# Two layers of graph attention on one core: where VectorE multiplies the context with the reciprocals

## The chip, the core and the metric

The kernel runs on one core of a Trainium2 chip. The core has engines with an instruction queue each, which work at the same time and wait for one another by semaphores: TensorE (PE, with the weight loads shown apart as PEld), VectorE (DVE), ScalarE (ACT), GpSimd (POOL) and SyncE (SP), which issues all of this kernel's DMAs. Inside a queue, instructions run strictly in the order in which the program wrote them. The metric is the device time of one execution in microseconds (us), the median of several runs.

## The reference

Two layers over x, of 8 elements (batch) x 2048 nodes x 256 features, with one 0/1 matrix `adj` of 2048 x 2048, each followed by a residual and a layer norm.

```python
# layer 0: per element, 4 heads of 64; keys in 8 chunks of 256
scores = einsum('bhnd,bhjcd->bhnjc', q, kc) / sqrt(Dh)
scores = clip(scores, -10, 10)
scores = where(mask == 0, -10, scores)
attn = softmax(scores, axis=-1)            # over the 256 keys of a chunk
ctx = einsum('bhnjc,bhjcd->bhnd', attn, vc)   # summed over the chunks
out = layernorm(ctx @ Wo.T + bo + x) * gamma + beta
x = layernorm(x + out)
# layer 1: per element, all 2048 keys
e = leaky_relu(s_i[:, :, None] + s_j[:, None, :], 0.2)
attention = softmax(where(adj > 0 or eye, e, -inf))
x = layernorm(x + elu(attention @ (x @ W)))
```

In layer 0 every chunk of 256 keys has a softmax of its own, so a chunk's part of the context is divided by that chunk's own sum, and the eight quotients are added.

## The kernel before

All arithmetic is in float32. Queries are taken in blocks of 512 (`ib`, four of them per element `b`), keys in chunks of 256 (`j`, eight of them). The main loop runs over J, the 8 x 4 x 8 = 256 triples (b, ib, j), and each J has two halves. A half is called a *beat*: it handles 128 keys against 512 queries for all heads, in two score tiles of 128 x 1024.

The order of the work is written out by hand. In a beat of the main loop the program writes, in this order:

1. `begin_beat` for layer 1: the exponentials of the steps that are due (`weights`, L727 on ACT), and with them the running sum of the weights (`acc`, L734 and L736 on POOL); the first instruction of new steps (`low`, L714 on ACT); and the second one of the steps begun a beat ago (`leaky`, L718 on DVE).
2. Layer 0's scores (L882 on PE), the clip against the mask (L893 on DVE, from PSUM in place), and the exponentials (L897 on ACT).
3. `middle_of_beat`: layer 1's mask (`edges`, L723 on DVE).
4. For the J before this one: the products of its exponentials with the values (L948 on PE). In the first half that is the denominators (part 2, against ones) and half the features, in the second the rest. ACT copies them out of PSUM: the features to `un` (L956), the denominators to `ds` (L962).
5. `end_beat`: layer 1's product (L746 on PE) and one step each of the generators in `ahead` (the preludes, which prepare layer 1 for an element; their row maxima are L438 on DVE) and `fins` (the output projection L357 with its norms, layer 1's end, and others). It then calls what stands in `agenda` for this beat; in the first element that is not over, and in the beats after the last scores, it calls the agenda ahead of the products and generators.

Denominators take a detour, since every head's row must be spread over 32 partitions. A DMA folds `ds` into the small tile `dc` (L964), DVE takes its reciprocal (`inverse`, L970), a DMA writes it to DRAM (L972), and a DMA reads it back spread over the partitions as `r` (`spread`, L976). Then `scaled` multiplies `un` by `r` on DVE (L983; L981 for a block's first chunk, which writes `ctxT` itself) and POOL adds the product to the context `ctxT` (L984).

From the second element on, `inverse` and `spread` stand at the end of the first half's beat and `scaled` at the end of the first half of the next J, two beats later. There the agenda holds `scaled` of one J in front of `inverse` of the next J, so that DVE's queue reads: ..., product, reciprocal, then the second half's L718, L893 and L723. In the first element, in which layer 1 does not run yet, all three come later.

A block's output projection may start in the beat after the one noted in `ctx_done`. Layer 1 takes 1.5 steps a beat, alternately one and two, of 128 keys against 512 queries; it begins when an element's layer 0 is done and its prelude has prepared it, and its weight tiles `w` have five buffers. `un` has two buffers.

Of the kernel before, what the change touches and what calls it, by code (L numbers as in the profile page):

```python
# [28 lines left out]
def tile_adj_attention__then__gat(  # L29
# [309 lines left out]
    ctx_done = {}  # L339
    fins = []  # L340
# [363 lines left out]
    class Step:  # L704
# [20 lines left out]
        def weights(self):  # L725
            k, c = self.k, self.c
            nc.scalar.activation(self.w, self.w, AF.Exp)  # L727
            if k["b"] == B - 1:
                return
            if c == 0:  # L730
                k["w0"] = self.w
            elif c == 1:
                k["acc"] = two.tile([P, IB], F32, tag="acc", name=f"acc{self.name}")
                nc.gpsimd.tensor_add(k["acc"], k.pop("w0"), self.w)  # L734
            else:
                nc.gpsimd.tensor_add(k["acc"], k["acc"], self.w)  # L736
# [65 lines left out]
    l1_live = True  # L802
    ahead = [prelude(b) for b in range(B - 1)] + [last_prelude(B - 1)]
    lows, edged, weighted = [], [], []
    agenda = {}
    beat = 0
    credit = 0.0
    RATE, LAST_RATE = 1.5, 1.3
# [1 line left out]
    def l1_open():  # L810
        return lows or edged or weighted

    def at(when, fn):
        agenda.setdefault(when, []).append(fn)

    def begin_beat(rate):
        nonlocal l1_live, credit, lows, edged, weighted, leaking
        weighted, edged = edged, []
        for s in weighted:
            s.weights()  # L820
        leaking, lows = lows, []
        credit = min(credit + rate, 2.0)
        while l1_live and credit >= 1.0:
            s = next(l1, False)
            if s is False:
                l1_live = False
            elif s is None:
                break
            else:
                credit -= 1.0  # L830
                lows.append(s)
                s.low()
        for s in leaking:
            s.leaky()

    def middle_of_beat():
        nonlocal edged
        for s in leaking:
            s.edges()
        edged = leaking  # L840

    def end_beat():

        nonlocal weighted
        if beat < 2 * NIB * NCH or beat >= 2 * total:
            for fn in agenda.pop(beat, []):
                fn()
        for s in weighted:
            s.product()
        weighted = []  # L850
        for gens in (ahead, fins) if beat < 2 * total else (fins, ahead):
            for g in list(gens):
                if next(g, g) is g:
                    gens.remove(g)
        for fn in agenda.pop(beat, []):
            fn()
# [14 lines left out]
    prev = None  # L871
# [28 lines left out]
    for J in range(total + 1):  # L900
        b, ib, j = J // (NIB * NCH), J // NCH % NIB, J % NCH
# [4 lines left out]
        for half in range(2):  # L906
            c = 2 * j + half
# [7 lines left out]
            if ahead_sc is not None:  # L915
                exponentials(cur, c, 0, ahead_sc)
            begin_beat(RATE if b < B - 1 else LAST_RATE)
            if live:

# [16 lines left out]
            early = J < NIB * NCH  # L936
            if prev is not None:
                if half == 0:

                    pool, tag = (one, "hr") if early and J % 3 == 2 else (two, "un")  # L940
                    prev["un"] = pool.tile([P, 2, IB], F32, tag=tag, name=f"un{prev['name']}")
                for part in ((2, 0), (1,))[half]:
                    m = ps_m.tile([P, IB], F32, tag="m", name=f"u{prev['name']}_{part}")
                    for i in range(2):
                        pc = 2 * prev["j"] + i
                        for h in range(H):
                            f0 = h * D + part * DH
                            nc.tensor.matmul(  # L948
                                m[h * DH : (h + 1) * DH, :],
                                prev["v"][pc // TPB][:, pc % TPB, f0 : f0 + DH] if part < 2 else ones[:, 0:DH],  # L950
                                prev["es"][2 * i + h // 2][:, h % 2, :],
                                start=(i == 0),
                                stop=(i == 1),
                            )
                    if part < 2:
                        nc.scalar.copy(prev["un"][:, part, :], m)  # L956
                    else:

                        ds = two.tile([P, IB], F32, tag="ds", name=f"ds{prev['name']}")
                        nc.scalar.copy(ds, m)  # L962
                        dc = two.tile([P, IB // DH], F32, tag="dc", name=f"dc{prev['name']}")
                        nc.sync.dma_start(  # L964
                            out=dc, in_=ds.rearrange("(h m) (n w) -> h m n w", m=DH, n=DH)[:, 0, :, :]
                        )
                        prev["dc"] = dc

                        def inverse(p=prev):
                            nc.vector.reciprocal(p["dc"], p["dc"])  # L970
                            p["rd"] = dram3.tile([H, IB], F32, tag="rd", name=f"rd{p['name']}")
                            nc.sync.dma_start(out=p["rd"].rearrange("h (m w) -> (h m) w", m=DH), in_=p["dc"])  # L972

                        def spread(p=prev):
                            p["r"] = two.tile([P, IB], F32, tag="r", name=f"r{p['name']}")
                            nc.sync.dma_start(out=p["r"], in_=p["rd"].unsqueeze(1).to_broadcast([H, DH, IB]))  # L976

                        def scaled(p=prev):
                            r2 = p["r"].unsqueeze(1).to_broadcast([P, 2, IB])
                            if p["j"] == 0:  # L980
                                nc.vector.tensor_mul(p["ctxT"], p["un"], r2)  # L981
                            else:
                                nc.vector.tensor_mul(p["un"], p["un"], r2)  # L983
                                nc.gpsimd.tensor_add(p["ctxT"], p["ctxT"], p["un"])  # L984
                            if p["j"] == NCH - 1:
                                ctx_done[p["b"], p["ib"]] = beat
                            if p["j"] == NCH - 3:
                                fins.append(fin(p["b"], p["ib"], p["ctxT"]))

                        lag = 1 if early else 0  # L990
                        at(beat + lag, inverse)
                        at(beat + lag, spread)
                        at(beat + 2 + 2 * lag, scaled)

            end_beat()
            if half == 1:
# [6 lines left out]
            beat += 1  # L1003
        prev = cur if live else None

    while agenda or fins or ahead or l1_live or l1_open():
        begin_beat(1.0)
        middle_of_beat()
        end_beat()
        beat += 1  # L1010
# [44 lines left out]
```

## Time and profile before

| what | value |
|---|---|
| time, median of 3 runs | 4385.68 us (4385.07 to 4389.45) |
| the profiled execution | 4386.54 us, its span 4384.7 us |
| mean granted TensorE clock | 0.979 |
| DMA traffic | 415.63 MB, mean 95 GB/s |
| reciprocals L970 | 256, of 0.25 us each |
| products L983 and L981 | 224 and 32; L983 has a mean of 1238 ns |
| context adds L984 | 224, mean 2535 ns |

A profile's row reads: line, engine, operation, output<-inputs with their shapes, count | busy us, mean ns of one | idle time of the engine just before, and what ended most of it. In a timeline the columns are start and duration in us, engine, line, operation, operands and count, and in brackets the idle time before and what ended it; neighbouring instructions of one line are merged. In the rows of windows the columns are the window, its length, and each engine's busy time with its number of instructions. A row of waits names who waited and for whom: us in total, times, the longest.

### The profile page before, as it was taken

The page shows a single profiled execution, that of the slowest core. Times are in us where ns is not written, and L with a number is a line of the kernel's source. Part 1 is how long each engine was busy: PE and PEld are TensorE (multiplying, and loading weights), DVE is VectorE, ACT ScalarE, POOL GpSimd, SP SyncE. Part 2 cuts the span into 40 slices and gives each one's busy share as a digit, 9 for nine tenths or more (in the row PEclk, how much of TensorE's full clock was granted, in tenths as well). Part 3 has the DMA queues.
Part 4 walks back from the last instruction along what each step waited for, and adds up shares of the span by engine and source line. Part 5 has one row for each costly group of instructions (what it writes and reads, how often), then busy time and mean ns, then how long its engine had stood idle before and what let it go on. Part 6 is the DMA issues. An engine that isn't in the chain of part 4 may idle for free.

```text
span 4384.7 us, 61166 instructions
## 1 busy us (share of the span) xinstructions
PE 4055.8 (92%) x23053; PEld 1913.0 (44%) x23053; DVE 3417.1 (78%) x4530; ACT 2555.5 (58%) x3842; POOL 1759.3 (40%) x901
## 2 busy tenths in 40 slices
PE   8889989999899999999899998999989999899767
PEld 3223334454345534454344543445434454344456
DVE  5876589965898668976699766996579965888777
ACT  5655556665566556666566665566556665555546
POOL 0222235543455434444245442554325542354420
PEclk9999999999999999999999999999999999999889
DMA  5554232223332133321333223222232222322321
GB/s 163 172 174 149 73 114 86 84 72 95 93 97 82 56 108 102 100 75 47 108 103 98 74 74 105 83 95 80 72 105 84 89 78 65 117 83 81 123 73 58
DMA packets 257642, 415.63 MB, mean 95 GB/s; under 512 B 85441, under 2 KB 120513, under 8 KB 256449
## 3 DMA queue, kind: packets, MB, share of 16 engines
q1 hardware_dynamic: 257344, 411.71, 30.7%
q8 instruction: 181, 2.97, 0.3%
q14 instruction: 117, 0.95, 0.1%
HBM read 340.66 MB, written 68.88 MB: 93 GB/s over the span
## 4 chain that ended last, share of the span: by engine, by line
PE 57%; DVE 23%; ACT 7%; DMA 7%; issue 5%; POOL 1%; SPq 0%; DVEq 0%; ACTq 0%; POOLq 0%
PE u L948 17%; PE sc L882 14%; PE us L746 12%; DVE sc L893 6%; DVE fb L438 3%; DVE w L718 3%; PE pv L275 3%; PE pk L256 3%; ACT e L897 3%; DMA dc<-ds 2%; PE pq L256 2%; DVE w L723 2%; PE po L357 2%; PE pw L398 2%; PE us L761 1%
## 5 line engine op out<-in xcount | busy, mean ns | idle before, releaser
L893 DVE SCALAR_TENSOR_TENSOR sc<-sc,mk 128x1024 f32<-128x1024 f32 x1024 | 1205.8, 1222 | 523.1 <-PE sc L882 375.0
L897 ACT ACTIVATE e<-sc 128x1024 f32<-128x1024 f32 x1024 | 1032.7, 1021 | 951.8 <-DVE sc L893 926.5
L882 PE MATMUL sc<-qT,kT 64*128 64x512 f32 x4096 | 1038.7, 622 | 71.8 <-ACT e L897 68.6
L984 POOL TENSOR_TENSOR ctxT<-ctxT,un 128x1024 f32<-128x1024 f32 x224 | 567.9, 2535 | 1135.6 <-DVE un L983 1099.8
L948 PE MATMUL u<-e,v 128*32 128x512 f32 x8192 | 982.8, 597 | 0.0
L746 PE MATMUL us<-wh,w 128*128 128x256 f32 x3584 | 883.0, 396 | 89.5 <-ACT w L727 68.2
L746 PEld LDWEIGHTS us<-wh,w 128*128 128x128 f32 x3584 | 669.8, 194 | 432.5 <-ACT w L727 119.7
L736 POOL TENSOR_TENSOR acc<-acc,w 128x512 f32<-128x512 f32 x392 | 600.0, 1531 | 548.1 <-ACT w L727 537.6
L882 PEld LDWEIGHTS sc<-qT,kT 64*128 64x128 f32 x4096 | 344.3, 186 | 581.3 <-issue 313.7
L718 DVE SCALAR_TENSOR_TENSOR w<-ab,sj,w 128x512 f32<-128x512 f32 x512 | 576.5, 1147 | 6.1 <-ACT w L714 6.1
L948 PEld LDWEIGHTS u<-e,v 128*32 128x32 f32 x8192 | 240.6, 110 | 659.8 <-issue 500.9
L948 PE MATMUL u<-e,ones 128*32 128x512 f32 x4096 | 498.4, 605 | 0.0
L723 DVE TENSOR_TENSOR w<-w,mk 128x512 f32<-128x512 f32 x512 | 458.5, 916 | 45.6 <-DMA mk<-mask 43.1
L438 DVE CUSTOM_DVE_ANT_0 fb<-sj_row,fb 128x1024 bf16<-128x1024 f32 x240 | 383.7, 1609 | 4.5 <-DMA fb<-far 4.5
L956 ACT COPY un<-u 128x512 f32<-128x512 f32 x512 | 300.7, 587 | 108.8 <-PE u L948 100.1
L714 ACT ACTIVATE w<-ab,sj 128x512 f32<-128x512 f32 x512 | 352.3, 715 | 9.9 <-POOL acc L734 5.2
L727 ACT ACTIVATE w<-w 128x512 f32<-128x512 f32 x512 | 308.8, 629 | 83.6 <-DVE w L723 83.2
L983 DVE TENSOR_TENSOR un<-un,r 128x1024 f32<-128x1024 f32 x224 | 277.2, 1238 | 43.6 <-DMA r<-rd 23.1
L948 PEld LDWEIGHTS u<-e,ones 128*32 128x32 f32 x4096 | 107.5, 110 | 352.7 <-issue 286.5
L970 DVE RECIPROCAL dc<-dc 128x16 f32<-128x16 f32 x256 | 63.5, 248 | 149.3 <-DMA dc<-ds 137.3
L962 ACT COPY ds<-u 128x512 f32<-128x512 f32 x256 | 148.6, 580 | 18.5 <-PE u L948 15.5
L357 PE MATMUL po<-WT_o,ctxT 128*128 128x256 f32 x512 | 127.4, 405 | 33.3 <-POOL ctxT L984 29.2
(112 smaller groups left out, 3078.7 us busy)
## 6 DMA issues: line engine op xcount, KB each, us to landing
r<-rd SPq DMA_DIRECT2D x256, 256.0 KB
mk<-mask SPq DMA_DIRECT2D x120, 512.0 KB
fb<-far SPq DMA_DIRECT2D x240, 256.0 KB
xT_k<-in_xT_dram SPq DMA_DIRECT2D x32, 512.0 KB
raw<-in_adjT_dram SPq DMA_DIRECT2D x32, 512.0 KB
rawf<-in_adj_dram SPq DMA_DIRECT2D x32, 512.0 KB
x<-in_x_dram SPq DMA_DIRECT2D x32, 512.0 KB
h_d<-y SPq DMA_DIRECT2D x32, 512.0 KB
```

What stands on the lines that cost most here:

```text
L438: nc.vector.tensor_tensor_reduce(out=fb, in0=row, in1=fb, scale=1.0, scalar=2 * FAR * 0.999, op0=ALU.add, op1=ALU.max, accum_out=dst,)
L714: nc.scalar.activation(self.w, k["ab"][:, 1, :], AF.Identity, bias=k["sj"][:, 1, c : c + 1])
L718: nc.vector.scalar_tensor_tensor(self.w, k["ab"][:, 0, :], k["sj"][:, 0, c : c + 1], self.w, ALU.add, ALU.max)
L723: nc.vector.tensor_tensor(self.w, self.w, self.k["mks"][self.c // HT][:, self.c % HT, :], ALU.min)
L727: nc.scalar.activation(self.w, self.w, AF.Exp)
L736: nc.gpsimd.tensor_add(k["acc"], k["acc"], self.w)
L746: nc.tensor.matmul(k["us"][:, t, :], self.w[:, ts(t, P)], k["wh"][c // TPB][:, c % TPB, 0:F], start=(first and t % 2 == 0), stop=last, ski ...
L882: nc.tensor.matmul(sc[:, h, :], kTs[b][n // TPB][h * D : (h + 1) * D, hp, ts(n % TPB, P)], qT[h * D : (h + 1) * D, hp, :], start=True, sto ...
L893: nc.vector.scalar_tensor_tensor(sc, sc, -CLIP, cap, ALU.max, ALU.min)
L897: nc.scalar.activation(e, sc, AF.Exp)
L948: nc.tensor.matmul(m[h * DH : (h + 1) * DH, :], prev["v"][pc // TPB][:, pc % TPB, f0 : f0 + DH] if part < 2 else ones[:, 0:DH], prev["es"] ...
L984: nc.gpsimd.tensor_add(p["ctxT"], p["ctxT"], p["un"])
```

## The change

`scaled` leaves the end of the beat for all chunks of which the denominators are made after the first element's scores. It is kept in a dictionary of its own, `scaling`, and is called in `begin_beat` of the next beat, behind all `leaky` calls of that beat and so in front of its clips. The running sum of layer 1's weights is split from `weights` into `sums`, which `begin_beat` calls after that; on GpSimd the context add therefore still comes in front of the same beat's weight adds. `ctx_done` is set one lower for the moved calls, so that the output projection is released in the same beat as before. Nothing else moves, and no instruction is added or taken away.

```diff
         def weights(self):
             k, c = self.k, self.c
             nc.scalar.activation(self.w, self.w, AF.Exp)
+
+        def sums(self):
+            k, c = self.k, self.c
             if k["b"] == B - 1:
                 return
             if c == 0:
...
-    agenda = {}
+    agenda, scaling = {}, {}
...
         for s in leaking:
             s.leaky()
 
+        for fn in scaling.pop(beat, []):
+            fn()
+        for s in weighted:
+            s.sums()
+
     def middle_of_beat():
...
                             if p["j"] == NCH - 1:
-                                ctx_done[p["b"], p["ib"]] = beat
+                                ctx_done[p["b"], p["ib"]] = beat if p["early"] else beat - 1
...
                         lag = 1 if early else 0
+                        prev["early"] = early
                         at(beat + lag, inverse)
                         at(beat + lag, spread)
-                        at(beat + 2 + 2 * lag, scaled)
+                        if early:
+                            at(beat + 2 + 2 * lag, scaled)
+                        else:
+                            scaling[beat + 3] = [scaled]
...
-    while agenda or fins or ahead or l1_live or l1_open():
+    while agenda or scaling or fins or ahead or l1_live or l1_open():
```

## The prediction

> **What bounds the kernel now.** I read the page's busy row, then the windows of one element (elements after the first repeat every 527 us; I use the third, 1005 to 1532 us), then what the reciprocals wait for, then the timeline around them.
>
> ```profile
> PE 4055.8 (92%) x23053; PEld 1913.0 (44%) x23053; DVE 3417.1 (78%) x4530; ACT 2555.5 (58%) x3842; POOL 1759.3 (40%) x901
> ...
> L718 DVE SCALAR_TENSOR_TENSOR w<-ab,sj,w 128x512 f32<-128x512 f32 x512 | 576.5, 1147 | 6.1 <-ACT w L714 6.1
> L983 DVE TENSOR_TENSOR un<-un,r 128x1024 f32<-128x1024 f32 x224 | 277.2, 1238 | 43.6 <-DMA r<-rd 23.1
> ```
>
> ```profile
> core 0: us, PE busy (x) PEld busy (x) DVE busy (x) ACT busy (x) POOL busy (x), PEclk, DMA share, GB/s
> 1005.00:1080.00 75.00, 72.48 (x439) 30.40 (x435) 38.97 (x58) 48.00 (x77) 23.05 (x11) 1.00 0.31 93
> 1080.00:1155.00 75.00, 62.83 (x415) 21.04 (x415) 62.01 (x88) 39.60 (x58) 23.57 (x10) 1.00 0.42 128
> 1155.00:1330.00 175.00, 168.05 (x947) 83.03 (x945) 168.18 (x206) 107.36 (x162) 92.95 (x48) 0.98 0.32 95
> 1330.00:1532.00 202.00, 198.51 (x1095) 103.03 (x1093) 147.85 (x192) 120.56 (x186) 93.40 (x51) 1.00 0.21 64
> ```
>
> PE is the bound, but not alone. From 1155 to 1330, where layer 1 runs beside the prelude's maxima (L438), DVE is as full as PE (168 of 175). In the first 150 us layer 1 stands still and PE idles 15 us in few, single waits. So a later clip (L893) costs time where PE waits for its exponential, and in the DVE-full stretch.
>
> ```profile
> DVE dc L970 <- DMA dc<-ds: 137.3, 98, 4.7
> ```
>
> The reciprocal is the DVE instruction that waits for the small transfer of the denominators. Now the product (L983) stands just in front of it and fills part of that wait.
>
> ```profile
> 1041.61 1.23 DVE L983 TENSOR_TENSOR un<-un,r 128x1024 f32<-128x1024 f32 x1 [5.21 <-ACT wh L399]
> ...
> 1044.44 0.25 DVE L970 RECIPROCAL dc<-dc 128x16 f32<-128x16 f32 x1 [1.60 <-DMA dc<-ds]
> 1044.61 2.33 DVE L893 SCALAR_TENSOR_TENSOR sc<-sc,mk 128x1024 f32<-128x1024 f32 x2
> ...
> 1045.85 1.02 ACT L897 ACTIVATE e<-sc 128x1024 f32<-128x1024 f32 x1 [2.48 <-DVE sc L893]
> ...
> 1046.77 0.58 ACT L956 COPY un<-u 128x512 f32<-128x512 f32 x1
> ...
> 1047.40 0.92 PE L398 MATMUL pw<-W_aug,hTl 128*128 128x258 f32 x3 [0.53 <-ACT un L956]
> ```
>
> Reciprocal, clip, exponential, copy, and PE waits for the copy: DVE's order reaches PE here without slack. Where layer 1 runs, POOL's adds meet DVE (DVE first, then POOL):
>
> ```profile
> 1290.31 0.25 DVE L970 RECIPROCAL dc<-dc 128x16 f32<-128x16 f32 x1 [1.06 <-DMA dc<-ds]
> 1290.48 1.76 DVE L718 SCALAR_TENSOR_TENSOR w<-ab,sj,w 128x512 f32<-128x512 f32 x1
> 1292.17 2.35 DVE L893 SCALAR_TENSOR_TENSOR sc<-sc,mk 128x1024 f32<-128x1024 f32 x2
> ...
> 1304.71 2.80 DVE L718 SCALAR_TENSOR_TENSOR w<-ab,sj,w 128x512 f32<-128x512 f32 x1
> ...
> 1319.87 0.67 DVE L718 SCALAR_TENSOR_TENSOR w<-ab,sj,w 128x512 f32<-128x512 f32 x1
> ...
> 1323.33 2.30 DVE L438 CUSTOM_DVE_ANT_0 fb<-sj_row,fb 128x1024 bf16<-128x1024 f32 x1
> ```
>
> ```profile
> 1289.33 2.36 POOL L984 TENSOR_TENSOR ctxT<-ctxT,un 128x1024 f32<-128x1024 f32 x1 [2.37 <-DVE un L983]
> 1291.66 3.08 POOL L736 TENSOR_TENSOR acc<-acc,w 128x512 f32<-128x512 f32 x2
> ...
> 1322.73 4.03 POOL L736 TENSOR_TENSOR acc<-acc,w 128x512 f32<-128x512 f32 x2
> ```
>
> L718 takes 0.66 us free and up to 2.8 when POOL's context add runs first. The clips pass under POOL's adds at their 1.2 us each; L438 does not (1.21 free, 2.30 under two adds).
>
> **The change part by part.** Nothing is added or removed; a product that waits for its spread reciprocals (r, 23.1 us in 4 waits) stands before the same clips in both orders. From the last chunk of the first element on, 225 products move on DVE from the end of a beat to behind the next beat's L718: past the reciprocal (L970) and one L718, rarely two. The order on PE, ACT and SP (its DMA issues included) stays. On POOL context add and weight adds keep their order too; only past the last scores do fins' adds (L349, L350, L606) come in front of a context add.
>
> *1. The wait loses its cover.* A transfer lands about 1.87 us after the copy of the denominators ends (L962 ends at 1288.44, the waiting reciprocal starts at 1290.31). The product covers 1.22 us less the 0.09 by which neighbours overlap: 1.13. Where the reciprocal waits today, it will start when it does now, and the product comes after it: clips 1.13 later. Where the transfer landed before the product began, nothing changes. In the window 991 to 1518, 14 of 32 wait (12 for 14.4 us on the transfer, 2 for 3.6 us labelled issue); by copy end plus 1.87, six more land during the product, three of those with L718 held to 2.8, and 12 are early.
>
> What reaches PE, read place by place. Without layer 1: the waiting reciprocals at 1005.97, 1044.44 and 1073.33 each lead by exponential and copy to a PE wait (PE at 1010.98, 1047.40, 1076.40): 3 x 1.13 = 3.4. At 1029.51 the clip waited 0.50 for PE anyway; some 0.3 is left. At 1056.75 the next clip waits 3.63 for PE: nothing, and 1.1 if that cover went. At 1087.94 a maximum held to 3.39 by POOL's L350 absorbs it; at 1139.87 a mask transfer does (L723 idle 6.17 before 1152.21). The output projection waits for the context add (PE 2.99 at 1104.44): 0.2 more, for the reciprocal now in front. Sum 3.8 to 3.9 an element, with bounds 0 and 6 x 1.13 = 6.8; I take 3.8, since the three PE waits name this chain. Seven elements: 27 us.
>
> [...]
>
> *2. POOL against DVE, with layer 1.* Where L718 was held, it falls from 2.80 to 0.66 (gain 2.1, less the 1.13 of step 1: clips 1.0 earlier) or from 1.76 to 0.66 (1.1, cancelling step 1). But then the context add takes the place under the clips that two weight adds had (1291.66), and these meet L723, L438 and L718: 1.1 to 1.2 us each, as at 1323.33. Where L718 was free (0.67 at 1319.87), the add was already under the clips: no change there but step 1. From 1155 to 1330: products at 1168.51 (+1.1) and 1183.45 (-1.0, then +2.4) are made good at a clip that waits 1.93 for PE; at 1216.66 by the output projection; at 1235.71 L723 waits for POOL's L370 in any case; at 1288.04, 1303.31 and 1318.56 (+2.4, then -1.0 +2.4, then +1.1) 4 us collect against 2.5 of DVE idle at 1330.47, and PE's scores wait up to 2 us. After 1330 clips wait 0.5 to 6 us for PE and cover it; in that cover's absence it would be a few us more. I take 2 us an element between -3 (three freed L718, no meeting) and +4, near the middle as the two prices are alike: 6.5 elements with layer 1, 13 us.
>
> [...]
>
> *3. Later weight adds.* They free the w buffers that L714 fills; ACT waits 5.2 us in all for L734 today. A second add some 4 us later (1298.9 for 1294.74) still ends before the L714 that reuses it: 0, and at most 0.1 us at each of ten products an element, 7 us. *4. The end.* The last context add (4137.31) goes behind L605, two L438, L606 and an L718; without the add those L438 (3.38, 3.36) shrink. y's addition (4148.22) comes out about 1 us later; between -3 and +6.
>
> Sum: 27 + 13 + 0 + 1 = 41. The profiled execution took 4386.5 (span 4384.7), 0.9 over the median 4385.7, so on the median: 4427.
>
> **The rivals.** *Faster: the freed L718 wins.* In 991 to 1518 nine L718 behind a reciprocal take over 0.7 us, 13.2 us too long in all; that is 13.2 x 6.5 = 86 of DVE's time. If the weight adds slip into DVE's short or PSUM instructions rather than in front of L438 and L718, the stretch 1155 to 1330 gains 3 us an element, minus step 1 at half: about 4366. For: L718's mean of 1147 against 0.66. Against: 1323.33, where adds behind the clips do hold L438. It decides from fewer than one meeting per moved add.
> *No change: all is covered.* PE is busy 198.5 of 202 us after 1330, and most clips there wait for PE. If the three PE waits of step 1 have slack that I miss, 4386. Against: they are waits in the record, with this chain in front.
> *Slower still: DVE's lag adds up.* If 4 us an element collect in the full stretch and later weight adds hold L714 in front of the exponentials, 27 becomes up to 47, 13 becomes 26: 4455 to 4461. For: DVE's 168 of 175; against: idle DVE of 2.5 us at 1330.
>
> **How the numbers follow.** Forecast case 0.62, faster 0.14, no change 0.13, slower still 0.11. About 0.2% (9 us) is what can be told from no change. Faster takes 0.14 of the first rival; same 0.13, most of the second and a little of the forecast's low edge; slower 0.73. The range leaves out the low end of the faster case and the tip of the high one: 4378 to 4461; the forecast case alone spans 4400 to 4450.
>
> **What would show it.** The reciprocals' wait for the transfer grows from 137 us towards 250 to 300. L718's mean falls below 1.1 us, with none held behind a reciprocal by L984, while L438 and L723 grow. PE's waits at the counterparts of 1010.98, 1047.40 and 1076.40 grow by 1.1 us each; PE's busy time stays at 4056. I am wrong if these grow and the time does not, or if L438 keeps 1.21 in the full stretch and PE's idle time shrinks.

## The result, and the profile after

The changed kernel takes 4451.21 us (median of five, 4445.38 to 4453.99) against 4389.45 for the kernel before (five runs, 4385.07 to 4394.53): a ratio of 1.0136, with an interval of 1.0124 to 1.0149. It is slower by about 60 us. The forecast was 4427, slower by 41, with a range of 4378 to 4461. The profiled execution took 4445.38 us, its span 4443.6, which is 58.9 longer than the span before. The code lines below have moved by three to eight: the reciprocal L970 is now L978, the product L983 is L991, the clip L893 is L901, the exponential L897 is L905, the copy L956 is L964, the context add L984 is L992, and the weight adds L736 are L739.

From the page of the changed kernel, the busy row and three groups:

```profile
PE 4082.4 (92%) x23053; PEld 1918.5 (43%) x23053; DVE 3413.4 (77%) x4530; ACT 2558.9 (58%) x3842; POOL 1729.9 (39%) x901
...
L718 DVE SCALAR_TENSOR_TENSOR w<-ab,sj,w 128x512 f32<-128x512 f32 x512 | 523.4, 1044 | 6.2 <-ACT w L714 6.0
L438 DVE CUSTOM_DVE_ANT_0 fb<-sj_row,fb 128x1024 bf16<-128x1024 f32 x240 | 419.1, 1757 | 1.5 <-DMA fb<-far 1.4
...
L991 DVE TENSOR_TENSOR un<-un,r 128x1024 f32<-128x1024 f32 x224 | 282.5, 1261 | 0.4 <-issue 0.4
```

DVE does no more work than before (3413 against 3417 us): L718 lost 53 us, and L438 (383.7 before) took 35 of them. PE, which has the same instructions, is busy 27 us longer. From the waits of the changed kernel:

```profile
DVE dc L978 <- DMA dc<-ds: 326.9, 141, 9.4
...
DVE w L723 <- DMA mk<-mask: 25.3, 10, 4.2
```

The reciprocals wait 190 us longer for the denominators than they did. Not all of that is new idle time: the products, which stood in front of them, had 43.6 us of idle time before them and now have 0.4, and VectorE's idle time as a whole (span less busy time) grew by 63 us, from 967.6 to 1030.2. The wait for the mask transfer (43.1 us before) became 18 us shorter. The windows of the changed kernel, for the same work as the four windows shown of before (bounds put at the same clips):

```profile
1017.30:1094.00 76.70, 71.39 (x433) 30.15 (x425) 39.86 (x59) 46.90 (x75) 22.14 (x11) 1.00 0.29 91
1094.00:1168.60 74.60, 64.74 (x416) 21.96 (x416) 61.15 (x89) 39.70 (x58) 23.35 (x10) 0.98 0.42 129
1168.60:1346.10 177.50, 168.25 (x948) 81.85 (x948) 166.90 (x205) 107.96 (x162) 92.12 (x48) 0.99 0.30 88
1346.10:1551.10 205.00, 200.52 (x1105) 104.44 (x1105) 148.09 (x194) 121.28 (x187) 92.18 (x51) 0.99 0.23 68
```

In this element the four stretches changed by +1.7, -0.4, +2.5 and +3.0 us. The second ends behind the element's first wait for a mask transfer, which gave back most of what the first two had lost; of the fourth the forecast had expected nothing.

**The step without layer 1.** The timeline of the changed kernel at the counterpart of 1044.44 to 1047.40:

```profile
1056.39 0.25 DVE L978 RECIPROCAL dc<-dc 128x16 f32<-128x16 f32 x1 [7.65 <-DMA dc<-ds]
1056.56 1.16 DVE L991 TENSOR_TENSOR un<-un,r 128x1024 f32<-128x1024 f32 x1
1057.64 2.35 DVE L901 SCALAR_TENSOR_TENSOR sc<-sc,mk 128x1024 f32<-128x1024 f32 x2
...
1058.90 1.02 ACT L905 ACTIVATE e<-sc 128x1024 f32<-128x1024 f32 x1 [3.19 <-DVE sc L901]
...
1059.82 0.58 ACT L964 COPY un<-u 128x512 f32<-128x512 f32 x1
...
1060.45 1.79 PE L398 MATMUL pw<-W_aug,hTl 128*128 128x258 f32 x7 [1.24 <-ACT un L964]
```

The product stands uncovered between reciprocal and clip, and PE waits 1.24 instead of 0.53. At the counterparts of the other two named waits, 1010.98 and 1076.40, PE waits 1.32 (0.22 before) and 1.85 (0.88). Three waits grew by 0.71 to 1.10 each, where 1.13 was forecast. (The 7.65 us ahead of the reciprocal hold the 5.21 us that stood ahead of the product in before.)

**With layer 1.** The timeline of before, from 1304.54 to 1330.47 (the L718 behind the first reciprocal takes 2.80 us and stands in the prediction):

```profile
1304.54 0.25 DVE L970 RECIPROCAL dc<-dc 128x16 f32<-128x16 f32 x1
...
1311.61 2.42 DVE L718 SCALAR_TENSOR_TENSOR w<-ab,sj,w 128x512 f32<-128x512 f32 x2
1313.95 2.35 DVE L893 SCALAR_TENSOR_TENSOR sc<-sc,mk 128x1024 f32<-128x1024 f32 x2
...
1319.70 0.25 DVE L970 RECIPROCAL dc<-dc 128x16 f32<-128x16 f32 x1
...
1330.47 2.36 DVE L893 SCALAR_TENSOR_TENSOR sc<-sc,mk 128x1024 f32<-128x1024 f32 x2 [2.51 <-PE sc L882]
```

The timeline of the changed kernel for the same J:

```profile
1320.94 0.25 DVE L978 RECIPROCAL dc<-dc 128x16 f32<-128x16 f32 x1 [1.15 <-DMA dc<-ds]
1321.11 0.66 DVE L718 SCALAR_TENSOR_TENSOR w<-ab,sj,w 128x512 f32<-128x512 f32 x1
1321.69 1.22 DVE L991 TENSOR_TENSOR un<-un,r 128x1024 f32<-128x1024 f32 x1
1322.82 2.36 DVE L901 SCALAR_TENSOR_TENSOR sc<-sc,mk 128x1024 f32<-128x1024 f32 x2
...
1325.81 2.29 DVE L438 CUSTOM_DVE_ANT_0 fb<-sj_row,fb 128x1024 bf16<-128x1024 f32 x1
...
1328.03 3.44 DVE L718 SCALAR_TENSOR_TENSOR w<-ab,sj,w 128x512 f32<-128x512 f32 x2
1331.40 2.35 DVE L901 SCALAR_TENSOR_TENSOR sc<-sc,mk 128x1024 f32<-128x1024 f32 x2
...
1337.14 0.25 DVE L978 RECIPROCAL dc<-dc 128x16 f32<-128x16 f32 x1 [1.06 <-DMA dc<-ds]
...
1346.58 2.35 DVE L901 SCALAR_TENSOR_TENSOR sc<-sc,mk 128x1024 f32<-128x1024 f32 x2
```

Here a loop can be read. A reciprocal is followed by the clips of its half, then by those of the next J's first half (1331.40). On ACT the denominators of that J are copied behind the exponentials of those clips (the copy runs from 1334.70 to 1335.28), the transfer lands 1.86 us later, and the next reciprocal can start. From the first half's clips to that reciprocal it is 5.74 us here, and 5.75 in before (1313.95 to 1319.70). From a reciprocal to the first half's clips it is 10.46 us here and 9.41 in before (1304.54 to 1313.95). The freed L718 takes 2.14 off that part (0.66 for 2.80), but the product adds 1.13, L438 1.08 (2.29 for 1.21, under the weight adds) and the pair of L718 1.02 (3.44 for 2.42). In before the product stood in the 5.75, beside ACT's work and the transfer; now it stands in the other part of the round, and DVE waits idle for the transfer instead. The J between these reciprocals takes 16.20 us against 15.16, the J ahead of it 16.30 against 14.23. In before the clips at 1330.47 waited 2.51 us for PE; their counterpart at 1346.58 waits for nothing. DVE's order, with the wait that it makes for itself, has become the pace there.

To follow the experiments, I split each element after the first by its clips and add up the seven elements from the trace: A is 11 J from the third on (layer 1 stands still), B the next 11 J (layer 1 beside the row maxima), and C the last 10 J up to the next element's third. The element's first wait for a mask lies at the start of B, so B returns a part of what A lost. The waits of the reciprocals are all idle time of DVE just ahead of them. All are us of the one profiled execution of each kernel; that of the changed kernel lay 6 us below its median and e12's 8 below, those of e1, e4 and e10 lay 9, 12 and 5 above.

| kernel | A | B | C | reciprocals wait in A / B / C | mask wait in B |
|---|---|---|---|---|---|
| before | 1030.4 | 1303.2 | 1310.9 | 79.5 / 9.2 / 42.2 | 40.3 |
| after | 1067.4 | 1308.1 | 1321.9 | 174.4 / 64.8 / 86.7 | 23.3 |
| e1 swap only | 1074.5 | 1304.4 | 1321.9 | 174.2 / 64.6 / 86.6 | 25.7 |
| e2 with layer 1 only | 1031.2 | 1323.1 | 1320.4 | 84.7 / 64.6 / 87.5 | 40.6 |
| e8 without layer 1 only | 1064.9 | 1287.3 | 1310.3 | 167.8 / 9.6 / 42.8 | 23.9 |
| e3 no split | 1067.1 | 1328.7 | 1355.3 | 171.7 / 64.2 / 89.1 | 24.3 |
| e4 reciprocal last | 1053.5 | 1278.4 | 1318.1 | 4.5 / 0 / 0 | 2.0 |
| e5 last, with layer 1 | 1033.4 | 1292.3 | 1318.1 | 69.0 / 0 / 0 | 40.2 |
| e6 the same, old product | 1031.6 | 1292.5 | 1315.7 | 69.4 / 0 / 0 | 38.0 |
| e7 behind the product | 1028.3 | 1292.9 | 1308.8 | 76.7 / 2.6 / 15.5 | 40.2 |
| e9 e7 without split | 1023.9 | 1323.4 | 1351.2 | 77.6 / 2.6 / 16.9 | 38.2 |
| e10 between the clips in A | 1038.4 | 1274.1 | 1307.1 | 12.1 / 2.6 / 15.3 | 1.3 |
| e11 between the clips everywhere | 1035.8 | 1274.0 | 1305.0 | 4.5 / 0 / 0 | 1.6 |
| e12 e7, mask a beat sooner | 1035.1 | 1264.9 | 1307.2 | 85.1 / 4.6 / 15.3 | 0 |

Two profiles of nearly the same stretch of code (the 470 us ahead of the first A) differ by up to 8.5 us, so single differences of a few us in this table say nothing.

### The profile page after: what moved, and what is told of

Read it like the earlier page. It is cut to its first block, busy times and chain, and to the rows that moved or that the text cites. A ratio compares the mean times of both kernels' runs of the same rounds, so it can differ in the third digit from the quotient of the medians.

```text
span 4443.6 us, 61096 instructions
## 1 busy us (share of the span) xinstructions
PE 4082.4 (92%) x23053; PEld 1918.5 (43%) x23053; DVE 3413.4 (77%) x4530; ACT 2558.9 (58%) x3842; POOL 1729.9 (39%) x901
## 5 line engine op out<-in xcount | busy, mean ns | idle before, releaser
L905 ACT ACTIVATE e<-sc 128x1024 f32<-128x1024 f32 x1024 | 1034.8, 1022 | 1027.7 <-DVE sc L901 1001.8
L901 DVE SCALAR_TENSOR_TENSOR sc<-sc,mk 128x1024 f32<-128x1024 f32 x1024 | 1207.7, 1224 | 456.6 <-PE sc L890 275.5
L890 PE MATMUL sc<-qT,kT 64*128 64x512 f32 x4096 | 1053.7, 627 | 97.5 <-ACT e L905 90.0
L992 POOL TENSOR_TENSOR ctxT<-ctxT,un 128x1024 f32<-128x1024 f32 x224 | 537.8, 2401 | 1410.2 <-DVE un L991 1384.6
L956 PE MATMUL u<-e,v 128*32 128x512 f32 x8192 | 979.3, 595 | 0.0
L739 POOL TENSOR_TENSOR acc<-acc,w 128x512 f32<-128x512 f32 x392 | 624.6, 1593 | 431.2 <-ACT w L727 418.1
L718 DVE SCALAR_TENSOR_TENSOR w<-ab,sj,w 128x512 f32<-128x512 f32 x512 | 523.4, 1044 | 6.2 <-ACT w L714 6.0
L956 PEld LDWEIGHTS u<-e,v 128*32 128x32 f32 x8192 | 240.1, 110 | 658.0 <-issue 494.8
L956 PE MATMUL u<-e,ones 128*32 128x512 f32 x4096 | 500.8, 607 | 0.0
L723 DVE TENSOR_TENSOR w<-w,mk 128x512 f32<-128x512 f32 x512 | 455.3, 911 | 27.8 <-DMA mk<-mask 25.3
L438 DVE CUSTOM_DVE_ANT_0 fb<-sj_row,fb 128x1024 bf16<-128x1024 f32 x240 | 419.1, 1757 | 1.5 <-DMA fb<-far 1.4
L964 ACT COPY un<-u 128x512 f32<-128x512 f32 x512 | 300.7, 587 | 102.9 <-PE u L956 94.9
L978 DVE RECIPROCAL dc<-dc 128x16 f32<-128x16 f32 x256 | 63.8, 249 | 345.5 <-DMA dc<-ds 326.9
L991 DVE TENSOR_TENSOR un<-un,r 128x1024 f32<-128x1024 f32 x224 | 282.5, 1261 | 0.4 <-issue 0.4
L956 PEld LDWEIGHTS u<-e,ones 128*32 128x32 f32 x4096 | 107.9, 110 | 355.2 <-issue 292.8
L970 ACT COPY ds<-u 128x512 f32<-128x512 f32 x256 | 148.7, 581 | 19.6 <-PE u L956 16.2
L357 PE MATMUL po<-WT_o,ctxT 128*128 128x256 f32 x512 | 127.4, 405 | 33.4 <-POOL ctxT L992 32.1
```

The source lines that it names most:

```text
L438: nc.vector.tensor_tensor_reduce(out=fb, in0=row, in1=fb, scale=1.0, scalar=2 * FAR * 0.999, op0=ALU.add, op1=ALU.max, accum_out=dst,)
L718: nc.vector.scalar_tensor_tensor(self.w, k["ab"][:, 0, :], k["sj"][:, 0, c : c + 1], self.w, ALU.add, ALU.max)
L723: nc.vector.tensor_tensor(self.w, self.w, self.k["mks"][self.c // HT][:, self.c % HT, :], ALU.min)
L890: nc.tensor.matmul(sc[:, h, :], kTs[b][n // TPB][h * D : (h + 1) * D, hp, ts(n % TPB, P)], qT[h * D : (h + 1) * D, hp, :], start=True, sto ...
L901: nc.vector.scalar_tensor_tensor(sc, sc, -CLIP, cap, ALU.max, ALU.min)
L905: nc.scalar.activation(e, sc, AF.Exp)
```

## The experiments

The medians stand beside runs of the kernel before on the same chip. Theory W says that the loss is the reciprocal's wait, which has lost the product as its cover. Theory P says that it is the meeting of GpSimd's adds with VectorE, as where L718 takes 2.80 us for 0.66: the change alters which instructions meet.

### e1: only the order of product and reciprocal

The kernel before, with the product behind the reciprocal at the same end of a beat; GpSimd's instructions keep the order of before.

```diff
-                        at(beat + 2 + 2 * lag, scaled)
+                        if early:
+                            at(beat + 2 + 2 * lag, scaled)
+                        else:
+                            behind[beat + 2] = scaled
...
         for fn in agenda.pop(beat, []):
             fn()
+        if beat in behind:
+            behind.pop(beat)()
```

> The kernel before, with one swap: at the end of the same beat the reciprocal stands ahead of the product, and both ahead of L718; GpSimd's adds keep their old order and place. Theory W (the loss is the reciprocal's wait that lost its cover, on DVE ahead of the clips): the wait for the small transfer grows to about 300 us as in the changed kernel, L718 gains nothing, and the time is at least that of the changed kernel: 4440 to 4480. Theory P (the loss is GpSimd's adds meeting DVE's instructions with two SBUF inputs, since the context add has moved under the clips): the context add runs ahead of the clips again and the weight adds under them, so little is lost: 4390 to 4412.

Measured: 4444.20 (4443.03 to 4453.17) against 4391.66; ratio 1.0123, interval 1.0107 to 1.0139. From its waits:

```profile
DVE dc L974 <- DMA dc<-ds: 330.5, 143, 10.1
```

The swap of two neighbours alone costs 52 us and brings the whole wait (330.5 for 326.9). That the product also passes an L718 and crosses into the next beat, and that the weight adds come later, makes the remaining 9 at most, and the two intervals meet. But e1 alone does not separate W from P. L718, which was expected to gain nothing, fell to 1061 ns on average (1147 in before) and L438 rose to 1743 (1609): with the product straight in front of L718, L718 begins before the context add does (at 1309.78 and 1309.95 us, for example). So the meetings changed here much as in the change. All together they give DVE no more work (busy 3406.9 us, 3417.1 in before); what they cost by their place is told apart by e8, e5 and e7.

### e2 and e8: the two parts apart

The order of the change only where steps of layer 1 are in flight (e2), and only where none are (e8, with the condition negated); elsewhere the order of before. The diff is that of e2.

```diff
+    def placed(p, fn):
+        p["moved"] = bool(lows or edged)
+        if p["moved"]:
+            scaling[beat + 1] = [fn]
+        else:
+            fn()
...
-                            scaling[beat + 3] = [scaled]
+                            at(beat + 2, lambda p=prev, fn=scaled: placed(p, fn))
```

> The changed order only in beats in which layer 1 has steps in flight, the old order in the others. By the prediction's terms (27 us without layer 1, 13 with it, 1 at the end) it takes 4385.7 + 14 = 4400. By the two traces, stage by stage (14 us without layer 1, 40 with it), it takes about 4430 to 4437. Theories W and P both allow either.

> The changed order only in beats without layer 1's steps; the counterpart of the run with it only in the others. If the two parts add up to the changed kernel's loss: about 4389 + 23 = 4412, which is also near the 27 us that the prediction put there. If the 37 us that the changed kernel's trace shows in these beats all count: 4426.

Measured: e2 4427.94 (4422.41 to 4432.19) against 4391.66, ratio 1.0081, interval 1.0065 to 1.0096: +36. e8 4416.13 (4410.12 to 4423.28) against 4393.34, ratio 1.0049, interval 1.0032 to 1.0066: +23. From the waits of e2:

```profile
DVE w L723 <- DMA mk<-mask: 42.0, 9, 6.4
```

From the waits of e8:

```profile
DVE w L723 <- DMA mk<-mask: 27.2, 10, 4.2
```

The two add up to 59, the loss of the whole change. e8 takes 34.5 us in A and gives 16 back in B, where DVE waits for the mask less than before (23.9 for 40.3). In e8 the meetings are those of before (L718 1145 and L438 1610 ns on average, 1147 and 1609 in before), so nothing but the order of reciprocal and product is left for its 23 us. e2 leaves the mask's wait as it was and loses 20 in B and 9.5 in C. So the part with layer 1 is the larger one, which the forecast had the other way round (27 and 13).

### e3 and e9: without the split of the weight adds

The change with the weight adds in front of the context add again (e3); and the same for e7, which is described below (e9).

```diff
             nc.scalar.activation(self.w, self.w, AF.Exp)
-
-        def sums(self):
-            k, c = self.k, self.c
             if k["b"] == B - 1:
...
-        for s in weighted:
-            s.sums()
```

> The changed kernel with the split undone: layer 1's weight adds are written at the head of the beat again, in front of the context add, so that they run as soon as the exponentials are there, beside DVE's wait. Theory P: most of the loss with layer 1 is regained: 4405 to 4425. Theory W: the wait stays at 300 us or more and so does the time: 4438 to 4455.

> The order of e7 (with layer 1 in flight L718, product, reciprocal, clips; without it the order of before), but the weight adds stand ahead of the context add again, as in before. It tells whether the later weight adds are needed because of the product's place or because of the reciprocal's. Theory A (the product in front of the clips runs under the weight adds on GpSimd, is held by them, and everything behind it on VectorE with it; so the split is the price of the product's place): 4405 to 4435, with the product's time above 1.4 us on average and the reciprocal's wait for the transfer below e7's 101 us, since the product ends later. Theory B (in the run with the split undone it was the product together with the reciprocal's uncovered wait in front of it): within 10 us of e7's 4376.

Measured: e3 4511.11 (4504.81 to 4515.68) against 4391.66, ratio 1.0270, interval 1.0254 to 1.0285, slower by 119. Both theories missed it: neither expected the split to matter that much. e9 4454.78 (4447.34 to 4457.10) against 4385.39, ratio 1.0165, interval 1.0149 to 1.0180: slower by 69, while e7, the same with the split, is faster than before. The two ratios of e9 and e7 are 2.0% apart, about 89 us. From the page of e9, the product:

```profile
L1002 DVE TENSOR_TENSOR un<-un,r 128x1024 f32<-128x1024 f32 x224 | 333.3, 1488 | 41.6 <-DMA r<-rd 41.5
```

The same row of e7:

```profile
L1008 DVE TENSOR_TENSOR un<-un,r 128x1024 f32<-128x1024 f32 x224 | 286.0, 1277 | 43.5 <-DMA r<-rd 31.2
```

A product in front of the clips runs while weight adds occupy GpSimd, and is held by them; L723 is held too (mean 1048 ns in e9, 917 in e7), and the context add comes later, so that PE's output projection waits for it longer (40.9 us against 31.8; in e3 55.6, against 32.1 in the changed kernel). Theory A of e9 had the direction, but half the size, and it was wrong that the reciprocal would wait less (107 us for 101). By their pages, PE's idle time grows by 40 us from e7 to e9 (span less busy time: 317.9 and 357.9) and its busy time by 32 with the same instructions; the section on the hardware comes back to that. So the second half of the change, the later weight adds, is no cost: without it the change would have lost twice as much.

### e4, e5 and e6: the wait taken away

In e4 the reciprocal stands behind the second half's clips, everywhere; in e5 only with layer 1 in flight; e6 is e5 with the product where it was in before.

```diff
     def middle_of_beat():
         nonlocal edged
+        for fn in inverting.pop(beat, []):
+            fn()
...
-                        at(beat + lag, inverse)
-                        at(beat + lag, spread)
...
+                            inverting[beat + 1] = [inverse, spread]
```

> The changed kernel, but the reciprocal stands behind the second half's clips instead of at the end of the first half; the product stays ahead of the clips. Theory W: the wait falls under 20 us, DVE reaches its clips earlier than in the kernel before, and the time is 4340 to 4390. Theory P: the context add stays under the clips and the weight adds behind it, so the loss with layer 1 stays: 4415 to 4440. A wait of the product for the spread reciprocals, which now leave some 3 us later, would show as idle time of DVE ahead of the product.

> Where layer 1 has steps in flight: L718, product, clips, reciprocal, as in the run with the reciprocal last. Elsewhere the order of the kernel before, so that the spread reciprocals are not late there. If that run lost 23 us without layer 1 by its products' wait for the spread reciprocals and gained 25 us in the full stretch by the vanished wait (as its stages say), this one takes 4355 to 4375, under the kernel before. If the full stretch's gain came from elsewhere: 4382 to 4395.

> As the run before this one, but the product stays at the end of the first half, where it stood before the change; only the reciprocal moves behind the clips, and only with layer 1 in flight. It differs from it by the product's place alone, with no reciprocal waiting in either. If the wait is all that the change is about (W): within 8 us of it, L718 held by the context add again. If freeing L718 is worth something by itself: 10 to 25 us longer.

Measured: e4 4389.42 (4385.40 to 4401.91) against 4391.66, ratio 0.9996, interval 0.9986 to 1.0006. e5 4390.05 (4378.50 to 4394.42) against 4393.34, ratio 0.9986, interval 0.9976 to 0.9997. e6 4386.15 (4382.45 to 4387.35), ratio 0.9979, interval 0.9969 to 0.9989. From the waits of e4:

```profile
DVE un L993 <- DMA r<-rd: 98.5, 27, 9.4
...
DVE dc L980 <- DMA dc<-ds: 24.1, 13, 4.0
```

With the reciprocal's wait gone, the loss is gone, though the product stays in front of the clips. e4 alone does not show W by that, since it gained at the mask as well (below). e5 beside e2 does: they differ by the reciprocal's place where layer 1 runs and by what follows from it on SyncE's queue, wait for the mask alike (40 us in B), and have nearly the same meetings (L718 1070 and 1044 ns, L438 1697 and 1737). The time goes from 36 us above before to 3 below, 31 us of it in B; in C e5 stays 7 above before, and no run shows why. In e4 the product waits for the spread reciprocals, 98.5 us against 23.1 in before, and A is 23 us longer than in before. I had read the 25 us that e4 gains in B as the reciprocal's wait, and so expected 4355 to 4375 of e5; it missed by 15 and more, since e5 does not have that gain. Its mask wait is 40 us and e4's 2, and only e12 told why. e6 beside e5 (4 us, intervals overlapping) says that the place of the product by itself is worth nothing that shows here; what counts is what covers the denominators. It does not price a freed L718: that was expected to be held again in e6, but took 1025 ns on average, since no reciprocal stands between it and the product any more.

### e7: the product in front of the reciprocal again

With layer 1 in flight: L718, product, reciprocal, clips. Without it the order of before. The split stays.

```diff
-        for fn in scaling.pop(beat, []):
+        for fn in scaling.pop(beat, []) + inverting.pop(beat, []):
             fn()
...
+    def moves():
+        return bool(lows or edged) and beat < 2 * total
+
+    def place_reciprocal(inverse, spread):
+        if moves():
+            inverting[beat + 1] = [inverse, spread]
+        else:
+            inverse()
+            spread()
```

> With layer 1 in flight: L718, product, reciprocal, clips. Both L718 and product now cover the reciprocal's wait, some 1.8 us instead of none in the changed kernel and 1.1 in the kernel before, so that of a wait of 2.2 us about 0.4 is left. W: between the kernel before and the run with the reciprocal behind the clips: 4365 to 4384. If the context add's new place under the clips costs by itself: over 4395.

Measured: 4376.16 (4370.47 to 4383.97) against 4393.34, ratio 0.9963, interval 0.9952 to 0.9974: faster than both kernels. The timeline of e7, for the same J as above:

```profile
1303.73 0.74 DVE L718 SCALAR_TENSOR_TENSOR w<-ab,sj,w 128x512 f32<-128x512 f32 x1
1304.40 1.21 DVE L1008 TENSOR_TENSOR un<-un,r 128x1024 f32<-128x1024 f32 x1
1305.53 0.24 DVE L995 RECIPROCAL dc<-dc 128x16 f32<-128x16 f32 x1
...
1308.54 2.30 DVE L438 CUSTOM_DVE_ANT_0 fb<-sj_row,fb 128x1024 bf16<-128x1024 f32 x1
...
1310.77 3.41 DVE L718 SCALAR_TENSOR_TENSOR w<-ab,sj,w 128x512 f32<-128x512 f32 x2
1314.10 2.35 DVE L918 SCALAR_TENSOR_TENSOR sc<-sc,mk 128x1024 f32<-128x1024 f32 x2
...
1320.51 0.23 DVE L995 RECIPROCAL dc<-dc 128x16 f32<-128x16 f32 x1
...
1330.98 2.36 DVE L918 SCALAR_TENSOR_TENSOR sc<-sc,mk 128x1024 f32<-128x1024 f32 x2 [2.83 <-PE sc L907]
```

L718 is free and the product still covers the denominators. From reciprocal to the first half's clips it is 8.57 us (10.46 in the changed kernel), the J takes 14.98, no reciprocal waits, and the clips at 1330.98 wait for PE again. L438 and the pair of L718 are held as in the changed kernel (2.30 and 3.41), so it is not these meetings that make the loss but the order of product and reciprocal. What makes e7 faster than before was not taken apart: e5, e6 and e7 all gain 10 to 11 us in B, and share shorter waits of the reciprocals, shorter L718, and 67 mask transfers that pass the denominators' DMAs on SyncE's queue because the reciprocal comes a beat later.

### e10, e11 and e12: where a reciprocal stands on SyncE's queue

e10 is e7, and where layer 1 stands still the reciprocal comes between the two clips of the second half. e11 puts it between the clips everywhere.

```diff
                     clip(sc, n)
+                    for fn in between.pop(beat, []):
+                        fn()
...
         if moves():
             inverting[beat + 1] = [inverse, spread]
+        elif beat < 2 * total:
+            between[beat + 1] = [inverse, spread]
```

> As e7, but where no layer 1 work is in flight the reciprocal stands between the two clips of the second half rather than ahead of both. The wait for the denominators in that stretch was 77 us in seven elements with e7, and the first clip then comes 1.2 us later behind it than it could. Theory W (the wait counts where PE waits for the exponential of the first clip, and the mask transfer gives part of it back): 4358 to 4370, with the wait in that stretch below 25 us and the idle time at the mask transfer up by 10 to 25 us. Rival M (the mask transfer sets the end of that stretch anyway): within 6 us of 4376, with the wait gone all the same.

> As e10, and also with layer 1 in flight the reciprocal stands between the two clips, with the product ahead of both. In e7 the reciprocals wait only 18 us in those two stretches, so the theory of the wait expects within 8 us of e10; a second clip 0.25 us later for the reciprocal costs nothing that shows. If more than the wait is at work there (the exponential of the first clip on the critical chain), it is faster than e10 by 8 to 20.

Measured: e10 4358.93 (4350.77 to 4364.05) against 4385.39, ratio 0.9943, interval 0.9930 to 0.9956. e11 4365.51 (4364.53 to 4366.94), ratio 0.9959, interval 0.9947 to 0.9972; as expected, no different from e10 by more than 8. The time of e10 is what W expected, but not the way there: A became 10 us longer (7 in e12, where DVE's order is that of e7), the product waits 71.9 us for its spread reciprocals (31.2 in e7), and the mask wait, which should have grown, vanished, with B 19 us shorter. SyncE's queue shows it. The timeline of e7:

```profile
1140.04 0.56 SPq L989 DMA_DIRECT2D dc<-ds  x1
1142.30 0.42 SPq L997 DMA_DIRECT2D rd<-dc  x1
1145.12 0.54 SPq L1001 DMA_DIRECT2D r<-rd  x1
1145.71 0.95 SPq L140 DMA_DIRECT2D mk<-mask  x2
```

The timeline of e10:

```profile
1139.33 0.56 SPq L993 DMA_DIRECT2D dc<-ds  x1
1141.58 1.21 SPq L140 DMA_DIRECT2D mk<-mask  x2
1143.10 0.32 SPq L1001 DMA_DIRECT2D rd<-dc  x1
1147.87 0.54 SPq L1005 DMA_DIRECT2D r<-rd  x1
```

In e7 the mask transfer with which an element's layer 1 begins is issued behind the write and the read of a denominator's reciprocal, so it waits for DVE's reciprocal and then for a DMA to land. In e10 the reciprocal was moved a beat on, and its two DMAs fell behind the mask's. e12 makes that move alone: e7 with the first mask of an element issued one beat sooner. Every other DMA, and every instruction of the four other engines, keeps the order of e7.

```diff
-                while ib not in st["ab"] or beat < st["ab"][ib][0]:
+                while ib not in st["ab"] or beat < st["ab"][ib][0] - 1:
                     yield None
                 mks = [mask_block(1, ib, 0, f"{b}_{ib}_0")]
+                while beat < st["ab"][ib][0]:
+                    yield None
```

> The order of e7, with one edit: the first mask transfer of an element's layer 1 is issued one beat sooner, so that on SyncE's queue it stands ahead of the copy and the spread of a denominator (both of which wait for a reciprocal) and not behind them. All instructions on the other four engines keep their order. e10 gained some 10 to 17 us over e7 by a reciprocal between the clips, and in its trace the mask transfer was issued 4.1 us sooner after the same copy of the denominators, because its issue no longer stood behind that reciprocal: so two causes changed in it at once. Theory Q (e10's gain was the mask transfer's issue freed on SyncE's queue; the reciprocal's wait ahead of the first clip had little to do with it): 4345 to 4364, the mask wait of 41 us below 8, and the reciprocal's wait as in e7 at 95 to 115 us. Theory W (the wait ahead of the first clip): 4370 to 4380, though the mask wait is gone.

Measured: 4359.57 (4351.70 to 4364.52) against 4395.21, ratio 0.9923, interval 0.9909 to 0.9936, the lowest ratio of all, though its interval meets e10's. From its timeline and its waits:

```profile
1134.88 0.42 SPq L140 DMA_DIRECT2D mk<-mask  x1
1136.75 0.56 SPq L991 DMA_DIRECT2D dc<-ds  x1
1140.32 0.32 SPq L999 DMA_DIRECT2D rd<-dc  x1
```

```profile
DVE dc L997 <- DMA dc<-ds: 114.2, 89, 4.5
```

Theory Q holds: the reciprocals wait as long as in e7 (114 us for the transfer, 101 in e7; in A 85 us of idle time for 77), no wait for the mask is left in B, and the time falls by 0.4% against e7 by the two ratios. So e10's gain over e7 needs no shorter wait of the reciprocal; the mask's place on the queue is enough. It also explains e4 and e5: e4 moved the reciprocals of A as well, and in its trace the mask is issued ahead of that write and read; in e5 it is issued behind them.

## Why the prediction was right, and where its sizes were off

The bound was read rightly: PE sets the pace, with few single waits in A, and DVE is as full as PE in B. Direction and mechanism held: e8 shows step 1 with GpSimd's meetings as in before, and e1 shows that the swap of the two neighbours is enough. 20 us were missing, a third of the loss.

**Step 1, the wait loses its cover (27 us).** The mechanism is as written, at the places named: the three PE waits of one element grew by 1.10, 0.71 and 0.97. Measured by e8 the term is 23 us; in its trace 34.5 are lost in A and 16 returned in B. The return at the mask had been named for one reciprocal; it took back about half. That the net came so near to 27 is partly luck: the loss in A was larger than the three waits named, and so was the return. The waits of all reciprocals, forecast to grow towards 250 to 300 us, grew to 326.9. Of the growth 43 us are idle time that stood ahead of the products before, and B and C have 56 and 44 us (9.2 to 64.8 and 42.2 to 86.7): with layer 1, in the J shown, DVE came to wait in every round for denominators that its own order delays.

The trace has 190 us more waiting ahead of the reciprocals and 59 us more span: most of the added wait is hidden elsewhere, as the step found at some of its places, or only changed its place.

**Step 2, POOL against DVE with layer 1 (13 us, bounds -3 to +4 an element).** This is the term that was mis-sized: e2 measured 36 us, 5.6 an element by the step's 6.5 elements, beyond its upper bound of 4. (The 2 us taken were called near the middle of -3 and +4, which is 0.5.) Its local prices were right: L718 fell from 2.80 to 0.66, L438 and the pair of L718 took 1.1 and 1.0 more under the weight adds, and between 1290.31 and 1330.47 about 3.1 us collected (reciprocals 16.30 and 16.20 us apart for 14.23 and 15.16), of which 1.3 came back at the clips. The failing sentences are those that let later waits repay. "After 1330 clips wait 0.5 to 6 us for PE and cover it": C lost 9.5 us in e2 and 11 in the change. And the places of B said to be made good were not all: B lost 20 in e2. The step counted GpSimd's meetings one by one, but did not follow the loop reciprocal, clips, exponentials, copy, transfer, reciprocal, in which the moved product lengthens every round. Over all the meetings cancel in DVE's busy time, with L718's 53 us against L438's 35 as the largest items: the cost is the wait, as e5 beside e2 and e7 show. In C that is less clear: no reciprocal waits there in e5, and its C stays 7 us above before, while e7's is 2 below.

**Step 3, later weight adds (0, at most 7).** ACT's wait for a `w` buffer is 6.0 us for 5.2 before: 0 was right. But the step priced only the delay of the adds. e3 and e9 show that it is an order worth some 60 to 90 us once the product stands in front.

**Step 4, the end (+1).** From the last clip to the end it is 275.1 for 272.5: +2.6, within its range.

**The rivals.** *Faster: the freed L718 wins* needed less than one new meeting per moved add; L438 kept 2.30 under the adds, and the reciprocal's wait ate the rest. Its own sum gives no 4366: 3 us in 6.5 elements, less half of step 1, is 6 us, so about 4380. e7, which keeps the cover and has the short L718, is faster than before, but how much of that is L718's was not measured. *No change* fell with the three PE waits. *Slower still* (4455 to 4461) came near in size, and its picture, DVE's lag that collects in B, is the one that the loop confirms; but not its split: the part without layer 1 became smaller than 27, not 47, and the part with it larger than 26.

**What would show it.** L718's mean fell below 1.1 (1044 ns), and L438 grew (1757 for 1609 ns). L723 did not (911 for 916 by the pages). PE's busy time was to stay at 4056 and became 4082, which no step had.

## What to carry to other kernels

Work that stands in front of a waiting instruction is the cover of that wait; moved behind it, it can cost about its whole duration in every round where the wait lies in a loop that feeds itself (here 1.22 us: the J shown takes 16.20 us in the changed kernel and 14.98 in e7, with the same meetings, and the product takes 1.22), and idle times seen later on that engine need not repay it (C lost 11 us in the change). When an order is changed to free one engine's conflict, keep the cover and move the waiting instruction along with it: that made a loss of 1.4% a gain of 0.4%. And read the DMA queue as one more engine in order: in e7 the mask transfer, issued at 1145.71 us behind two others that wait for a reciprocal, waited for it too, and its issue a beat sooner was worth as much again (ratio 0.9963 in e7, 0.9923 in e12).

## What the runs showed of the hardware

**PE waits more and is busy longer too.** In the changed kernel PE idles 32 us longer than in before (span less busy time: 361.2 and 328.9), and is busy 27 us longer with the same 23053 matmuls. The granted clock can explain part of that: in the clock records of before it is 0.50 in 32 stretches (19 of 3.41 us, 8 of 6.83), in those of the changed kernel in 42 (25 and 14). In before the matmuls of L948 take 1061 ns on average inside these stretches and 597 outside; in the changed kernel they (L956) take 1060 and 597. Within the span 91 us of full-speed time are lost by it in before (mean granted clock 0.979) and 107 in the changed kernel (0.976). 10 of these 15 us lie in C, where before loses none. From e7 to e9, with 40 us more idle time, the loss goes from 90 to 122 (mean clock 0.979 and 0.972). But e2 is 36 us slower with a loss of 91 (0.979), as in before, and e4 loses 112 (0.975) with PE's idle time as in before (329.3), so the two do not go together always; with one profile of each kernel, how it divides stays open. What brings such a stretch on was not tried.

**The first of two adds decides who is held.** With the weight adds in front, in e9, the product is held (1488 ns on average against 1277 in e7) and L438 less (1542 against 1707); with the context add in front, in e7, it is the other way round. The sum differs: DVE's busy time is 93 us longer in e9 than in e7 (3489.7 and 3396.3), with the same instructions.
